# A scan layer with mixture-of-experts and flow attention: the first stage's order of work cut to single time steps

## The chip, the cores and the metric

The kernel runs on one core of one Trainium2 chip. The time is what the device needs for one execution, in microseconds (us). The kernel before takes 5714.69 us (median of 3 runs, 5713.19 to 5721.97). One further execution was recorded by the profiler; it took 5735.0 us, of which 5733.2 us lie between its first and its last instruction (the span). All rows quoted are from that execution.

The engines are named as the profile names them: PE is TensorE (PEld its weight loads), DVE VectorE, ACT ScalarE, POOL GpSimd, SP the engine whose queue issues the DMAs. [...]

## The reference

For x of 8 x 1024 x 256 in float32, four layers follow, each added to its input: a Mamba block, experts, a flow attention, and the same experts again. The first stage of the kernel computes the first two.

```python
xn = layernorm(x);  x_in, z = split(xn @ in_proj_w.T + in_proj_b)
x_conv = silu(causal_conv4(x_in))                  # 512 channels
Bm, Cm = split(x_conv @ x_proj_w.T + x_proj_b)     # 16 states each
delta  = clip(softplus(x_conv @ dt_proj_w.T + dt_proj_b), 1e-4, 10)
# for each time step t:
h = exp(clip(delta * A, -10, 0)) * h + delta * Bm * x_conv
# after every 16th step: h scaled down where its norm over the states is over 10
y = sum_n(Cm * h) + D_param * x_conv
out = layernorm(x + (y * silu(z)) @ out_proj_w.T + out_proj_b)
# experts: 16 of 256 x 256, the router's best 6 weighted, all 16 computed
out = sum_e(gate[:, e] * (tokens @ expert_w[e]))
```

## The kernel before

Stage one runs over 1024 time steps with all 8 batches at once. A partition holds one pair of batch and state (8 x 16 = 128), the free axis the 512 channels, so h is one tile of 128 x 512. The scan cannot be spread over time: each step (`step`, L545) is two instructions on DVE, `tmp = max(E, exp(-10)) * h` (L550) and `h = tmp + px` (L552). Everything else prepares or uses what the scan needs, and is woven between the steps:

- E = exp(delta * A). The deltas of 16 steps go to DRAM (L452, 256 KB) and come back spread over the states (`load_E`, 1 MB for a group of 4 steps, 3 buffers). POOL multiplies by A one step at a time (`mul_E`, L501) and ACT takes the exponential of four steps at once (`exp_E`, L505).
- px = B*u, one product per step with 32 rows (`inputs`, L537). The four steps of a group use four row groups of the array and four PSUM banks; a bank comes free when the step that reads it is done.
- py = C*h, four products per group in four column groups of the array, one bank (`outputs`, L581). `take_y` copies the bank out after 16 steps.
- after every 16th step the norm: ACT squares h, PE sums over the states, ACT takes logarithm and exponential, DVE scales h (`norm_a`, `norm_b`, `clip`).
- `pre(sc)` makes the inputs of the scan for a chunk of 32 steps (256 rows of tokens): normalisation, input projection, convolution, and the projections to B, C and delta; `gates(sc)` makes the gate z and both SiLUs, for which ACT loads another table. `weights(j)` builds the operands of B and C.
- `post(sc)` takes a finished chunk through the output projection, two normalisations and the router. `experts1(sc)` runs the 16 experts over both halves of the 256 tokens: two experts per PSUM bank (128 x 512, L707), read out by DVE (L727) for six of eight pairs and by ACT (L733) for two.

PSUM has 8 banks: four for px, one for py, and three that all other products share in turn (`psum()`, pool `ps_g`).

The order is written out by hand (`manual_schedule`). The main loop goes over groups of 4 steps; `PLAN` says after which step of which group of a chunk one part of the generators `ahead` (pre, letter a), `mid` (post, m) or `behind` (experts, b) is issued, and g calls `gates`. A generator's part ends at its `yield`. What a part issues goes to the end of each engine's queue, so a waiting instruction holds up all that its engine was given later. In the window from 200 to 3900 us 936 steps are recorded, 3.953 us a step or 126.5 us a chunk. Stage two (attention and the second experts) begins at about 4165 us and is not touched.

Of the kernel before, what the change touches and what calls it, by code (L numbers as in the profile page):

```python
# [17 lines left out]
P = 128  # L18
# [14 lines left out]
def tile_mamba_moe_flowattn_moe(ctx: ExitStack, tc: tile.TileContext, a: dict, out: bass.AP):  # L33
# [174 lines left out]
    with ExitStack() as ph:  # L208
# [8 lines left out]
        ps_g = ph.enter_context(tc.tile_pool(name="ps_g", bufs=3, space=PSUM))  # L217
# [115 lines left out]
        def pre(sc):  # L333
# [28 lines left out]
            for k in range(KD):  # L362
                for g in range(2):
                    nc.tensor.transpose(tp[:, k * 256 + g * P:k * 256 + (g + 1) * P],
                                        xn[:, g, k * P:(k + 1) * P], ident)
            xT = t["xT"] = io.tile([P, KD, HC + T * B], F32, tag="xT", name="xT")
# [12 lines left out]
            acc2 = t["acc"] = []  # L379
            prev = None  # L380
            for c in range(CB + 1):
                if c < CB:
                    ps = psum()
                    for k in range(KD):
                        nc.tensor.matmul(ps[:, 0:HC + T * B], inw[:, k, c * P:(c + 1) * P], xT[:, k, :],
                                         start=k == 0, stop=k == KD - 1)
                    if c % 2 == 0:
                        acc2.append(act.tile([P, 2, T * B], F32, tag="e", name="acc"))
                    acc = acc2[c // 2][:, c % 2, :]
                    nc.scalar.activation(acc, ps[:, 0:T * B], AF.Identity, bias=cbi[:, c:c + 1], scale=cw[:, c, 0:1])  # L390
                if prev is not None:
                    pps, pacc = prev
                    for k in range(1, 4):
                        nc.vector.scalar_tensor_tensor(pacc, pps[:, k * B:(k + T) * B], cw[:, c - 1, k:k + 1], pacc,  # L394
                                                       ALU.mult, ALU.add)
                    if sc == 0:
                        for i in range(3):
                            nc.vector.tensor_scalar(pacc[:, i * B:(i + 1) * B], pacc[:, i * B:(i + 1) * B],
                                                    cws[:, c - 1, 2 - i:3 - i], None, ALU.subtract)
                prev = (ps, acc)  # L400
                yield

            xc = t["xc"]
# [6 lines left out]
            dps = [psum(), None]  # L410
            for k in range(CB):
                nc.tensor.matmul(dps[0], tok(xc, k, 0), dtw[:, k, :], start=k == 0, stop=k == CB - 1)  # L412
            yield
            nc.vector.tensor_tensor(bc, bps[:, 0:4 * NS].rearrange("p (g n) -> p g n", g=2),
                                    xpb.unsqueeze(1).to_broadcast([P, 2, 2 * NS]), ALU.add)
            vs, es, ws = [], [], []
            for g in range(2):
                v = act.tile([P, DI], F32, tag="v", name="v")
                nc.vector.tensor_tensor(v, dps[g], dtb, ALU.add)
                e = act.tile([P, DI], F32, tag="e", name="e")  # L420
                nc.scalar.activation(e, v, AF.Abs)
                nc.scalar.activation(e, e, AF.Exp, scale=-1.0)
                w = act.tile([P, DI], F32, tag="w", name="w")
                nc.scalar.activation(w, e, AF.Identity, bias=1.0)
                vs.append(v), es.append(e), ws.append(w)
                if g == 0:
                    dps[1] = psum()
                    for k in range(CB):
                        nc.tensor.matmul(dps[1], tok(xc, k, 1), dtw[:, k, :], start=k == 0, stop=k == CB - 1)  # L429
                yield  # L430


            xcts = []
            for g in range(2):
                v, e, w = vs[g], es[g], ws[g]
# [3 lines left out]
                nc.vector.scalar_tensor_tensor(w, w, -1.0, e, ALU.add, ALU.subtract)  # L439
                nc.scalar.activation(e, e, AF.Ln, bias=1.0)  # L440
                nc.vector.scalar_tensor_tensor(v, v, 0.0, w, ALU.max, ALU.subtract)
                xct = act.tile([P, DI], F32, tag="xct", name="xct")
                nc.scalar.copy(xct, tp)
                xcts.append(xct)
                yield
            for g in range(2):
                v, e = vs[g], es[g]
                nc.gpsimd.tensor_tensor(v, v, e, ALU.add)
                nc.gpsimd.tensor_scalar(v, v, 10.0, 1e-4, ALU.min, ALU.max)
                c = ch_tiles[2 * sc + g] = {}  # L450
                c["dt"] = dbc.tile([4, B, QS, DI], F32, tag="dbc", name="dbc")
                nc.sync.dma_start(c["dt"].rearrange("q b tg d -> tg (q b) d"), v)  # L452
                yield
                u = c["u"] = act.tile([P, DI], F32, tag="u", name="u", bufs=3)
                nc.gpsimd.tensor_tensor(u, v, xcts[g], ALU.mult)
                if g == 1:
                    yield
# [5 lines left out]
        def gates(sc):  # L463

            t = sc_tiles[sc]
            xc = t["xc"] = act.tile([P, CB, 2, 4, 4, B], F32, tag="xc", name="xc")
            zs = t["zs"] = act.tile([P, CB, 2, 4, 4, B], F32, tag="zs", name="zs")
            zps = []
            for j in range(2):
                ps = psum()  # L470
                for i in range(2):
                    m = CB + 2 * j + i
                    for k in range(KD):
                        nc.tensor.matmul(ps[:, i * 256:(i + 1) * 256], inw[:, k, m * P:(m + 1) * P],
                                         t["xT"][:, k, HC:], start=k == 0, stop=k == KD - 1)
                zps.append(ps)
            acc = t.pop("acc")
            for dst, of, src in ((xc, lambda c: acc[c // 2][:, c % 2, :], "acc"),
                                 (zs, lambda c: zps[c // 2][:, c % 2 * 256:(c % 2 + 1) * 256], "z")):
                for c in range(CB):  # L480
                    for g in range(2):
                        nc.scalar.activation(
                            dst[:, c, g], of(c)[:, g * P:(g + 1) * P].rearrange("p (t4 tg b) -> p tg t4 b", t4=4, tg=4),
                            AF.Silu, bias=inb[:, CB + c:CB + c + 1] if src == "z" else 0.0)
            nc.scalar.preload_act_table_set("natural_log_exp_and_others")

# [4 lines left out]
        def load_E(G):  # L491
            if G < NQ:
                E_of[G] = scn.tile([P, QS, DI], F32, tag="E", name="E", bufs=3)
                j, q = divmod(G, 4)
                src = ch_tiles[j]["dt"][q].rearrange("b tg d -> b (tg d)")
                nc.sync.dma_start(E_of[G].rearrange("p tg d -> p (tg d)"),
                                  src.unsqueeze(1).to_broadcast([B, NS, QS * DI]))

        def mul_E(G, i):
            if G < NQ:  # L500
                nc.gpsimd.tensor_tensor(E_of[G][:, i, :], E_of[G][:, i, :], A_bn, ALU.mult)  # L501

        def exp_E(G):
            if G < NQ:
                nc.scalar.activation(E_of[G], E_of[G], AF.Exp)  # L505

        def weights(j):

            if j >= NQ // 4:
# [9 lines left out]
                                    bc[:, g, NS:].unsqueeze(1).to_broadcast([P, B, NS]), ALU.mult)  # L519
            ps = psum()  # L520
            nc.tensor.matmul(ps, cm.rearrange("p b n -> p (b n)"), sel.rearrange("p s t q b -> p (s t q b)"),
                             start=True, stop=True)
            lC = c["lC"] = scn.tile([P, 4, 4, 32], F32, tag="lC", name="lC")
            nc.scalar.copy(lC.rearrange("p q t m -> p (q t m)"), ps)

        def inputs(G):
# [6 lines left out]
            x_of[G] = []  # L533
            for tg in range(4):
# [3 lines left out]
                x_of[G].append(ps)  # L538
# [6 lines left out]
        def step(G, tg):  # L545
            if tg == 0:
                h_of[G] = []
            tmp = scn.tile([P, DI], F32, tag="tmp", name="tmp")

            nc.vector.scalar_tensor_tensor(tmp, E_of[G][:, tg, :], math.exp(-10.0), last[0], ALU.max, ALU.mult)  # L550
            h = scn.tile([P, DI], F32, tag="h", name="h", bufs=6)
            nc.vector.tensor_tensor(h, tmp, x_of[G][tg], ALU.add)  # L552
            h_of[G].append(h)
            last[0] = h
            if tg == 3:
                E_of.pop(G), x_of.pop(G)

        def norm_a(G):
            sq = scn.tile([P, DI], F32, tag="tmp", name="sq")
            nc.scalar.activation(sq, last[0], AF.Square)  # L560
            clips[G] = sq

        def norm_b(G):
# [3 lines left out]
            nc.tensor.matmul(ps, blk, sq, start=True, stop=True)  # L567
            nc.scalar.activation(sq, ps, AF.Ln, bias=tiny)
            nc.scalar.activation(sq, sq, AF.Exp, scale=-0.5, bias=ln10)

        def clip(G):
            nc.vector.scalar_tensor_tensor(last[0], clips.pop(G), 1.0, last[0], ALU.min, ALU.mult)  # L572
# [20 lines left out]
        def post(sc):  # L593
# [6 lines left out]
            tps = []  # L600
            for j in range(2):
                tp = psum()
                for i in range(2):
                    for g in range(2):
                        c = 2 * j + i
                        nc.tensor.transpose(tp[:, i * 256 + g * P:i * 256 + (g + 1) * P],
# [427 lines left out]
```

## Time and profile before

| | |
|---|---|
| median of 3 runs | 5714.69 us |
| profiled execution, its span | 5735.0 us, 5733.2 us |
| stage one, to the last store of `x2` | about 4165 us |
| PE, DVE, ACT, POOL busy over the span | 85%, 65%, 32%, 47% |
| granted TensorE clock over the span | 0.849 |

The page gives busy times per engine, the span in slices, the queues, the chain of work that ended last, and the groups of instructions. Busy time of PE is stretched where the granted clock is low: a matmul at half clock counts twice. The answers about waits name the waiting instruction, the one that released it, the sum, the number of times and the longest.

### The profile page before, as it was taken

Reading aid. Unit: us, or ns where it says so; the run is one execution under the profiler, and the core shown is the slowest. Engines: PE = TensorE matmul, PEld = TensorE weight load, DVE = VectorE, ACT = ScalarE, POOL = GpSimd, SP = SyncE. Lnnn points to the kernel's source line nnn. Section 1 sums busy time; section 2 is a strip of 40 time slices with the busy share of each in tenths; the row PEclk is TensorE's granted clock in tenths of the full one; section 3 lists DMA queues with packets and bytes.
Section 4 is the critical chain, followed back from the end, with each engine's and each line's share of the span. In section 5 each row is a group of like instructions: output and inputs, shape, how many; then the busy total and the mean of one; then the engine's idle time right before and its main releaser. Section 6 shows DMA issues by size and latency. Waiting matters only on the chain.

```text
span 5733.2 us, 47074 instructions
## 1 busy us (share of the span) xinstructions
PE 4864.5 (85%) x14024; PEld 2136.7 (37%) x14024; DVE 3731.1 (65%) x7655; ACT 1858.5 (32%) x3234; POOL 2684.9 (47%) x2431
## 2 busy tenths in 40 slices
PE   4788888888888888888888888888968889888999
PEld 2233333333333333333333333333334444444444
DVE  3677766666777676667776776676656665656563
ACT  3333333333333333333333333333222223222322
POOL 3555554555555555555555555555423333333333
PEclk7678788878887878878878887787989999999999
DMA  3333332333333333333333333333100000000000
GB/s 104 89 78 78 77 78 71 78 78 79 76 79 76 75 75 78 79 76 76 78 77 74 76 78 77 76 77 79 48 23 6 13 13 13 6 13 13 6 6 10
DMA packets 100926, 339.13 MB, mean 59 GB/s; under 512 B 11584, under 2 KB 58816, under 8 KB 67904
## 3 DMA queue, kind: packets, MB, share of 16 engines
q1 hardware_dynamic: 100672, 336.12, 23.9%
q8 instruction: 113, 1.85, 0.1%
q14 instruction: 141, 1.16, 0.1%
HBM read 302.54 MB, written 33.55 MB: 59 GB/s over the span
## 4 chain that ended last, share of the span: by engine, by line
PE 52%; DVE 30%; ACT 6%; issue 4%; POOL 4%; DMA 2%; SPq 1%; DVEq 0%; ACTq 0%; POOLq 0%
PE po L170 14%; PE pg L707 10%; DVE tmp L550 9%; DVE h L552 6%; PE px L537 6%; PE pg L412 3%; DVE o L727 2%; PE py L581 2%; ACT E L505 2%; PE mm L886 2%; PE pg L429 2%; PE mm L859 2%; DVE rc L913 2%; PE pg L625 1%; DVE acc L394 1%
## 5 line engine op out<-in xcount | busy, mean ns | idle before, releaser
L501 POOL TENSOR_TENSOR E<-E,A_bn 128x512 f32<-128x512 f32 x1024 | 1401.2, 1388 | 1001.9 <-DMA E<-dbc 870.9
L537 PE MATMUL px<-u,lB 32*128 32x512 f32 x2048 | 935.3, 785 | 423.6 <-DVE h L552 419.9
L707 PE MATMUL pg<-ew,xmT 128*128 128x512 f32 x2048 | 1154.9, 701 | 0.6 <-DVE o L727 0.6
L550 DVE SCALAR_TENSOR_TENSOR tmp<-E,h 128x512 f32<-128x512 f32 x1024 | 959.3, 937 | 27.5 <-ACT E L505 2.6
L170 PE MATMUL po<-ew,xmT 128*128 128x512 f32 x2048 | 914.9, 595 | 7.4 <-ACT sc__23342 L180 0.6
L552 DVE TENSOR_TENSOR h<-tmp,px 128x512 f32<-128x512 f32 x1024 | 703.8, 687 | 84.7 <-PE py L581 2.1
L707 PEld LDWEIGHTS pg<-ew,xmT 128*128 128x128 f32 x2048 | 441.7, 226 | 610.2 <-issue 597.8
L727 DVE SCALAR_TENSOR_TENSOR o<-pg,gt,o 128x256 f32<-128x256 f32 x768 | 369.5, 481 | 407.1 <-PE pg L707 393.2
L537 PEld LDWEIGHTS px<-u,lB 32*128 32x128 f32 x2048 | 247.6, 217 | 928.1 <-DVE h L552 803.0
L505 ACT ACTIVATE E<-E 128x2048 f32<-128x2048 f32 x256 | 486.9, 1902 | 294.6 <-POOL E L501 294.6
L170 PEld LDWEIGHTS po<-ew,xmT 128*128 128x128 f32 x2048 | 384.1, 191 | 459.1 <-issue 421.2
L174 DVE SCALAR_TENSOR_TENSOR x2t<-po,gt,x2t 128x256 f32<-128x256 f32 x512 | 244.3, 477 | 380.6 <-PE po L170 372.5
L581 PE MATMUL py<-h,lC 128*32 128x512 f32 x2048 | 377.0, 705 | 33.7 <-DVE h L572 33.7
L913 DVE RECIPROCAL rc<-mm 128x512 f32<-128x512 f32 x64 | 212.6, 3341 | 22.3 <-PE mm L859 22.3
L633 POOL TENSOR_TENSOR s<-s,phalf 128x2 f32<-128x2 f32 x32 | 34.2, 1070 | 375.1 <-DVE s L632 375.0
L394 DVE SCALAR_TENSOR_TENSOR acc<-pg,cw,acc 128x256 f32<-128x256 f32 x384 | 184.9, 482 | 21.8 <-ACT acc L390 12.7
L321 ACT ACTIVATE x<-xr,nb,r 128x256 f32<-128x256 f32 x64 | 35.0, 593 | 468.7 <-DVE nb L316 468.7
L581 PEld LDWEIGHTS py<-h,lC 128*32 128x32 f32 x2048 | 52.0, 118 | 341.6 <-issue 260.0
L620 POOL TENSOR_TENSOR x<-x,out_proj_b_r 128x512 f32<-128x512 f32 x32 | 40.9, 1278 | 292.5 <-ACT x L321 292.5
L859 PE MATMUL mm<-ke,wt 128*128 128x512 f32 x128 | 82.4, 781 | 108.3 <-DVE wt L856 101.6
L657 PE MATMUL pg<-rw,xmT 128*128 128x16 f32 x256 | 57.9, 366 | 131.5 <-ACT xmT L653 131.5
L79 DVE BATCH_NORM_STATS2 st<-o 128x6 f32<-128x256 f32 x128 | 52.6, 411 | 169.6 <-POOL o L639 168.5
(1066 smaller groups left out, 6465.8 us busy)
## 6 DMA issues: line engine op xcount, KB each, us to landing
E<-dbc SPq DMA_DIRECT2D x256, 1024.0 KB
dbc<-v SPq DMA_DIRECT2D x64, 256.0 KB
xt<-in_x_dram SPq DMA_DIRECT2D x256, 32.0 KB
xr<-in_x_dram SPq DMA_DIRECT2D x256, 32.0 KB
x<-o SPq DMA_DIRECT2D x256, 32.0 KB
x2t<-x SPq DMA_DIRECT2D x8, 1024.0 KB
out_dram<-x2t SPq DMA_DIRECT2D x32, 256.0 KB
ew<-in_expert_w_dram SPq DMA_DIRECT2D x2, 2048.0 KB
```

The costliest lines, as they stand in the source:

```text
L170: nc.tensor.matmul(po, xmT[:, k, g * P:(g + 1) * P], ew[:, k, 2 * j:2 * j + 2, :], start=k == 0, stop=k == KD - 1)
L174: nc.vector.scalar_tensor_tensor(xr[:, g, :], po[:, i, :], gt[:, g, 2 * j + i:2 * j + i + 1], xr[:, g, :], ALU.mult, ALU.add)
L394: nc.vector.scalar_tensor_tensor(pacc, pps[:, k * B:(k + T) * B], cw[:, c - 1, k:k + 1], pacc, ALU.mult, ALU.add)
L501: nc.gpsimd.tensor_tensor(E_of[G][:, i, :], E_of[G][:, i, :], A_bn, ALU.mult)
L505: nc.scalar.activation(E_of[G], E_of[G], AF.Exp)
L537: nc.tensor.matmul(ps, lB[r, q * P:(q + 1) * P], c["u"][r, :], start=True, stop=True)
L550: nc.vector.scalar_tensor_tensor(tmp, E_of[G][:, tg, :], math.exp(-10.0), last[0], ALU.max, ALU.mult)
L552: nc.vector.tensor_tensor(h, tmp, x_of[G][tg], ALU.add)
L581: nc.tensor.matmul(c["ps"][tg * 32:(tg + 1) * 32, :], c["lC"][:, q, tg, :], h_of[G][tg], start=q == 0, stop=q == 3)
L707: nc.tensor.matmul(po, xmT[:, k, g * P:(g + 1) * P], ew[:, k, 2 * j:2 * j + 2, :], start=k == 0, stop=k == KD - 1)
L727: nc.vector.scalar_tensor_tensor(o[:, g, :], po[:, i * D:(i + 1) * D], gt[:, g, 2 * j + i:2 * j + i + 1], o[:, g, :], ALU.mult, ALU.add)
L913: nc.vector.reciprocal(rc, ps)
```

## The change

The loop goes over time steps instead of groups of four. After each step one expert's product (128 x 256, two matmuls) and at most one short group of other products are issued, as a `PLAN` with one entry per step of a chunk says (a: pre of the next chunk, p: pre of the one after, m: post, w and W: weights, c: take_y, e: an expert, after every step).

- Experts: one per step, in turn in the two halves of a PSUM tile of its own, `pe` (one bank). The product of expert n is issued, then the read-out of expert n-1. The shared banks go from three to two. ACT reads out experts 4, 5, 10 and 11 of each half. The router's part moves from `experts1` into `post`.
- `inputs`: px of the last step of the next group is issued first. The pool hands out its four banks in the same turn as before, so this px takes the bank that the step just issued is still to read, and the other three wait behind it on PE.
- E in tiles of 2 steps (512 KB, 6 buffers): a load every second step, the multiplication 7 steps ahead (before: 6), the exponential of 2 steps, 4 steps ahead (before: 2).
- `gates` becomes part of `pre`; `pre`, `post` and `weights` get more and shorter parts. In `pre` the third and fourth input products are issued behind the convolution that frees their bank.
- The norm and the clip work in two halves of 256 columns.

```diff
+        ps_e = ph.enter_context(tc.tile_pool(name="ps_e", bufs=1, space=PSUM))
+        ps_g = ph.enter_context(tc.tile_pool(name="ps_g", bufs=2, space=PSUM))
+        pe = ps_e.tile([P, 2, D], F32, name="pe")
...
             for c in range(CB + 1):
+                if c > 0:
...
+                    nc.scalar.activation(acc, ps[:, 0:T * B], AF.Identity, bias=cbi[:, c - 1:c],
+                                         scale=cw[:, c - 1, 0:1])
+                    if prev is not None:
+                        conv(sc, c - 2, *prev)
+                    prev = (ps, acc)
                 if c < CB:
                     ps = psum()
...
+            for c in range(CB):
+                silu(xc, acc2[c // 2][:, c % 2, :], c, 0.0)
+            for c in range(CB):
+                silu(zs, zp[c // 2][:, c % 2 * 256:(c % 2 + 1) * 256], c, inb[:, CB + c:CB + c + 1])
+            nc.scalar.preload_act_table_set("natural_log_exp_and_others")
+            yield
...
-            for tg in range(4):
+            x_of[G] = {}
+            for tg in (3, 2, 1, 0):
                 ps = ps_x.tile([P, DI], F32, tag="x", name="px")
...
+            for n in range(2 * NE + 1):
+                g, e = divmod(n, NE)
+                if n < 2 * NE:
+                    po = pe[:, n % 2, :]
+                    for k in range(KD):
+                        nc.tensor.matmul(po, xmT[:, k, g * P:(g + 1) * P], ew[:, k, e, :],
+                                         start=k == 0, stop=k == KD - 1)
+                if before is not None:
+                    side = evict(o, gt, sm, side if e != 1 else None, *before)
...
+                before = (g, e, po)
+                yield
...
+        PLAN = ("cm", "m", "", "ma",
+                "a", "aa", "aW", "m",
+                "ma", "ma", "ma", "mw",
+                "mwa", "am", "a", "amp",
+                "ca", "am", "ap", "ap",
+                "a", "a", "p", "am",
+                "apW", "mw", "wm", "mp",
+                "mp", "mp", "mpp", "mp")
...
+            if t < L:
+                step(G, tg)
+            mul_E(t + 7)
+            if tg % 2 == 0:
+                exp_E(t // 2 + 2)
+            else:
+                load_E(t // 2 + 6)
+            if tg == 3:
+                if clipped:
+                    norm_a(G)
+                inputs(G + 1)
+                if clipped:
+                    norm_b(G)
+            for who in PLAN[n] + ("ee" if n == 31 else "e"):
...
+            if clipped:
+                clip(G)
+            if tg == 3 and G < NQ:
                 outputs(G)
```

## The prediction

> **What bounds the kernel now.** First the busy times by stretch, to see whether an engine is full. Columns: busy us of PE, PEld, DVE, ACT, POOL with counts, granted clock, DMA share, GB/s.
>
> ```profile
> 1000.00:2000.00 1000.00, 848.96 (x2460) 352.92 (x2460) 695.25 (x1295) 357.21 (x576) 543.69 (x432) 0.81 0.32 78
> 4600.00:5733.00 1133.00, 1033.75 (x2939) 513.62 (x2937) 622.18 (x1708) 293.13 (x660) 386.16 (x512) 0.96 0.03 10
> ```
>
> In stage one DVE is busy for 0.695 of the time: of the 126.5 us of a chunk 87.9 are work and 38.6 idle. PE looks fuller but runs at a mean clock of 0.81. So no engine is full; queues wait for each other. Next, what DVE waits for (window 200 to 3900, 29.25 chunks; us in total, times, longest):
>
> ```profile
> DVE o L727 <- PE pg L707: 347.2, 97, 6.7
> DVE st L79 <- POOL o L639: 157.4, 29, 6.7
> DVE bc L414 <- PE pg L408: 156.2, 29, 6.5
> DVE v L419 <- PE pg L412: 134.5, 29, 5.5
> DVE lg L660 <- PE pg L657: 115.0, 29, 4.0
> DVE h L572 <- ACT sq L569: 53.4, 30, 4.2
> ```
>
> Per chunk: 11.9 us for experts' products, 19.3 for the next four together, 1.8 for the clip, some 5.6 in gaps. The scan itself (L550, L552) waits for E or px hardly at all. Third, the clock, in windows of 3.41 us:
>
> ```profile
> 2010.02:2013.44 3.42, 1.89 (x10) 0.80 (x8) 3.30 (x7) 0.90 (x2) 0.00 (x0) 1.00 0.18 57
> 2013.44:2016.85 3.41, 3.41 (x10) 0.95 (x12) 3.31 (x5) 1.94 (x4) 2.94 (x3) 0.53 0.52 111
> 2091.94:2095.36 3.42, 1.60 (x7) 0.34 (x5) 3.22 (x3) 0.93 (x3) 2.71 (x2) 1.00 0.49 108
> 2095.36:2098.77 3.41, 3.41 (x11) 2.06 (x11) 3.17 (x6) 1.69 (x1) 0.00 (x0) 0.53 0.40 99
> 2218.24:2221.65 3.41, 2.15 (x10) 0.40 (x9) 2.68 (x2) 1.07 (x3) 3.38 (x3) 1.00 0.48 113
> 2221.65:2225.06 3.41, 2.70 (x11) 1.35 (x12) 3.10 (x6) 2.38 (x2) 0.29 (x1) 1.00 0.37 102
> ```
>
> After a window with 1.60 or 1.89 us of PE work the clock halves for the next one; after 2.15 it stays. In the chain of waits:
>
> ```profile
> 2023.60 1.81 PE px L537 x2
> 2043.67 3.73 PE pg L707 x4
> 2063.58 3.41 PE pg L707 x4
> 2143.09 3.01 PE pg L707 x4
> ```
>
> Four matmuls of L707 take about 1.75 us at full clock and a px 1.12. Adding up what such pieces lose in the chunk from 2023.6 to 2150.5 gives 13.8 us. At full clock the chunk would need about 113.
>
> **Edits with one answer.** E moves the same bytes. ACT does 512 exponentials of 1024 columns for 256 of 2048: rows of 0.63 us (512 columns) and 1.90 (2048) leave a fixed 0.20, so 256 x 0.20 = 51 us on ACT, which is idle 65%; without that cover 51 us. SP issues 256 more loads of 0.61 us, 156 us on a queue that stood 2224 us waiting for a scan step to free an E buffer. The queue also carries the moved loads of x (8 behind step 15, 8 behind step 0), the stores of x2 (behind 16 and 31, waiting for POOL) and the deltas (behind 18 and 24). 8 loads have taken 15 us behind an E load; such a hold delays E. Behind it stand POOL's multiplications, but loads now lead them by 4 steps (before 3) and the scan by 11, and 512 KB take half of today's 8.5 us. I take nothing; uncovered it is one late load a chunk, some 5 us. The clip in halves costs DVE the same (0.96 us against two of 0.48).
>
> An expert takes 4 matmuls of 256 columns. Stage two has that shape: 37.8 us for 160 of L900, 0.236 each, 0.945 an expert, against 4 x 0.446 / 2 = 0.89 by L170 (704.6 for 1579). 1024 experts x 0.05 = 56 us on PE, behind DVE's work; uncovered 56. PE's work at full clock is some 80 us a chunk.
>
> **What it removes.** The four DVE waits of 19.3 us a chunk: each reader now comes in a later step than its product. About 2 may stay: -17.3. **px:** four together have taken 1.14 us (like a pair), apart 3.65 a group on average (935.3 / 256). That is PE time, which bounds nothing by itself; but all four now start only after the group's last h.
>
> **What it adds: the coupling of PE and DVE.** An eviction today reads one of three rotating banks; no row shows DVE reading a bank that PE has next to write. The nearest row is L552 on its own four banks, with 0.08 us of idle a step. The Trainium skill (*PSUM — Partial Sum Buffer*, "PSUM bank collisions raise a hardware error") says that two engines must be kept apart by bank and quadrant, not by address. `pe` is one bank. So I take it that the program makes read-out n-1 wait for product n, issued just ahead of it, and product n+1 for that read-out. Each wait is zero or the excess of PE's path over DVE's own work; scan step 1.65 us (0.94 + 0.69), eviction 0.5, expert to readable result 1.09 (0.945 + 0.15 tail), semaphore 0.05.
>
> - A fourth step, behind 19: h at 1.65, px holds PE to 2.66, the delta product 0.88, expert 1.09, 0.05: 4.68. DVE has 1.65 + 1.4. Wait 1.6. Likewise behind 3, 15, 23 and 31 (with their norms and products): 1.05, 0.7, 2.5, 0.3. Sum 6.2.
> - The step after, behind 8: PE is free 0.25 late (py 0.95), then L625 0.94, L408 1.0, expert 1.09, 0.05 = 3.33 against 1.65: 1.7. Behind 0, 4, 9, 13, 16, 20: 1.1, 0.7, 0.7, 1.75, 0.45, 0.65. Sum 7.05.
> - Two shared banks: the third input product waits for the convolution of the same step (DVE 1.65 + 1.6 + 1.45 = 4.7), then 0.94 + 1.09 + 0.05 = 6.8: wait 2.1 behind 29, 1.15 behind 30.
> - Behind 6, ACT gets 16 SiLUs and two table loads, 6.4 us in the row of before, ahead of the read-out of expert 5. Product 7 waits for that read-out, every DVE read-out behind it: 6.3 us. The same rows already held up L408 today.
>
> Sum 22.9 in place of 11.9. The chunk at full clock is 87.9 + 22.9 + 2 + 1.8 + about 3.6 of gaps = 118. If the halves were independent, the first three would shrink to about 3 and the SiLUs' to 6: 104. I take the whole wait, by the rule, with 104 as the other end.
>
> **The clock after.** PE's work is spread more evenly, but five stretches of a chunk stay thin: behind steps 1 to 2 (2.5 us of work in 8), 6 to 7, 17 to 18, 29 to 30 and 31. What follows runs at half clock: px, a product and an expert lose about 1.0 + 0.9 + 1.0, some on cover; I take 2.2 each, 11 us. The skill (*TensorE: Matmul & The Clock Gate*, Part 1) has the clock halved after an idle window of about 3.4 us. The window fits, but the rows above halve after 1.60 and 1.89 us of work. By the page only a pause as long as a window costs, almost nothing here: 118 a chunk. By the rows 118 + 11 = 129, which I take.
>
> **Sum.** 129 - 126.5 = +2.5 us over 30 chunks with experts: +75. After the scan 64 steps remain with experts alone. They took about 95 us (4064 to 4159). Now product and read-out alternate, at best 1.09 + 0.05 + 0.5 = 1.65, at half clock up to 2.7; at 1.95 it is 125: +30. 5735 + 105 = 5840 for the profiled execution. The median lies 0.35% below it: **5820 us**, 1.8% slower. 0.2% is about what a measurement of this kernel can tell from no change.
>
> **Rivals.**
> 1. Slower, as above: chance 0.56. Its own range is 5730 to 6010: 6010 if every thin stretch halves the clock on the path (some 134 a chunk: +225, and +50 at the end).
> 2. The clock holds, as the page has it, and the removed waits win: 118 + 3 = 121 a chunk, -5.5 x 30 + 30 = -135: 5580. For it: an expert behind every step leaves no long pause. Against it: the threshold near 2 us of 3.41 in the rows. It decides once the half-clock loss falls below 7 us a chunk. Chance 0.28.
> 3. No wait by bank: 104 + 6 = 110, -16.5 x 30 = -495: 5220. For it: nothing in the profile is against it. Against it: the rule. Chance 0.12.
> 4. The gains and the new waits cancel within 0.2%: 5703 to 5726, 126.5 less 1 a chunk for the longer end. Chance 0.04.
>
> So faster 0.40, same 0.04, slower 0.56. Cases of both signs hold most of the chance, so the range reaches into rival 2 and to the edge of 3: 5380 to 6000, leaving about 0.11 below and 0.08 above.
>
> **What the changed profile would show.** Right: DVE's waits for bc, v, lg and st near zero; evictions waiting for the experts' product about 23 us a chunk or more, largest behind every fourth step and around the SiLUs; px in fours of 1.14 or 2.08 us behind h; a clock of about 0.85 in stage one; POOL seldom waiting for E. Wrong: evictions that hardly wait (rival 3), or a clock above 0.95 (rival 2). E arriving late, or DVE's own rows lengthening, would break the sum elsewhere.

## The result and the profile after

The changed kernel takes **5934.34 us** (median, 5926.35 to 5940.5), the kernel before 5716.88 us beside it: a ratio of 1.038 (95% interval 1.0361 to 1.0397), so 3.8% slower. The forecast was 5820 us, 1.8% slower: the right side, about half the size. The profiled execution took 5940.5 us (span 5938.8), 205.5 us more than before's 5735.0.

Where they lie: the last clip of the scan ends at 4245.0 us (before 4090.6), and stage two's first work on DVE starts at 4375.6 (before 4170.3). So the scan takes 154.4 us longer and the tail of experts behind it 50.9 us (130.6 for 79.7). Together they are the whole difference. From first to last h the scan takes 129.3 us for 32 steps, before 124.5.

What DVE waits for, in the same window as before (200 to 3900 us; us in total, times, longest):

```profile
DVE o L759 <- PE pe L743: 975.4, 376, 8.0
DVE top L711 <- ACT lg L703: 49.8, 27, 3.4
DVE s L357 <- POOL s L355: 30.6, 28, 1.1
DVE h L575 <- PE px L559: 18.1, 36, 1.3
DVE st L79 <- POOL o L674: 10.0, 23, 0.4
```

The four waits that the change was to remove (bc, v, lg, st: 563 us together) are gone but for some 16 us, most of it at st; new ones, for the exponential of the router's logits (top) and for POOL (s), are 80. The wait for experts' products rose from 347 to 975 us. In this window 897 steps are recorded, 132.0 us a chunk, of which these waits are 34.8.

The clock, in windows of 3.41 us. Columns: busy us of PE, PEld, DVE, ACT, POOL with counts, granted clock, DMA share, GB/s.

```profile
2016.85:2020.26 3.41, 1.72 (x8) 1.05 (x6) 3.38 (x5) 1.06 (x1) 3.41 (x4) 1.00 0.15 45
2020.26:2023.67 3.41, 3.41 (x8) 1.29 (x8) 3.34 (x7) 0.00 (x0) 1.43 (x1) 0.61 0.21 65
2023.67:2027.09 3.42, 3.42 (x7) 1.68 (x6) 0.81 (x2) 0.00 (x0) 0.00 (x0) 0.50 0.52 128
2027.09:2030.50 3.41, 3.41 (x18) 1.95 (x17) 2.02 (x3) 0.00 (x0) 2.11 (x2) 0.89 0.53 131
```

One thin window (1.72 us of PE work) is followed by some 7 us at half clock. Six stretches at half clock, of 3.4 to 10.2 us, lie between 2013 and 2144 us; stage one's mean clock is 0.83 (before 0.81). The work alone does not decide it: here is a fuller window, mostly px with its 32 rows, and the one behind it.

```profile
2065.39:2068.80 3.41, 2.82 (x10) 0.91 (x9) 3.08 (x5) 0.23 (x1) 3.33 (x3) 1.00 0.01 2
2068.80:2072.21 3.41, 3.41 (x6) 1.63 (x6) 3.10 (x8) 0.49 (x2) 3.29 (x4) 0.50 0.47 126
```

The timeline around the longest wait of that chunk, behind step 6 (start, duration, engine, line; in brackets the idle time ahead and who ended it):

```profile
2039.55 1.13 PE L658 MATMUL pg<-outw,yT 128*128 128x256 f32 x4 [1.54 <-ACT zs L406]
2042.37 2.07 PE L743 MATMUL pe<-ew,xmT 128*128 128x256 f32 x4 [1.69 <-ACT side L764]
...
2041.84 0.47 ACT L764 ACTIVATE side<-pe,gt 128x256 f32<-128x256 f32 x1
...
2044.48 0.48 DVE L759 SCALAR_TENSOR_TENSOR o<-pe,gt,o 128x256 f32<-128x256 f32 x1 [7.57 <-PE pe L743]
```

ACT's read-out stands behind the SiLUs, product 7 behind it, and DVE behind the product for 7.57 us. But PE itself stood at the product for only 1.69 us: until shortly before, it had waited for the SiLUs in another place (L658, for the bank of z).

### The profile page after: what moved, and what is told of

Read it like the earlier page. It is cut to its first block, busy times and chain, and to the rows that moved or that the text cites. A ratio compares the mean times of both kernels' runs of the same rounds, so it can differ in the third digit from the quotient of the medians.

```text
span 5938.8 us, 52317 instructions
## 1 busy us (share of the span) xinstructions
PE 4924.3 (83%) x16200; PEld 2544.5 (43%) x16200; DVE 3790.6 (64%) x7719; ACT 1918.4 (32%) x3682; POOL 2758.0 (46%) x2431
## 5 line engine op out<-in xcount | busy, mean ns | idle before, releaser
L743 PE MATMUL pe<-ew,xmT 128*128 128x256 f32 x4096 | 1280.9, 442 | 292.5 <-DVE o L759 166.1
L743 PEld LDWEIGHTS pe<-ew,xmT 128*128 128x128 f32 x4096 | 859.6, 222 | 718.1 <-DVE o L759 302.0
L759 DVE SCALAR_TENSOR_TENSOR o<-pe,gt,o 128x256 f32<-128x256 f32 x768 | 369.4, 481 | 1156.1 <-PE pe L743 1154.9
L559 PE MATMUL px<-u,lB 32*128 32x512 f32 x2048 | 817.1, 801 | 122.1 <-DVE h L575 119.4
L523 ACT ACTIVATE E<-E 128x1024 f32<-128x1024 f32 x512 | 537.6, 1051 | 201.8 <-POOL E L519 201.8
L750 POOL TENSOR_TENSOR o<-o,side 128x256 f32<-128x256 f32 x128 | 122.3, 956 | 538.3 <-DVE o L759 531.9
L448 PE MATMUL pg<-dtw,xc 128*128 128x512 f32 x512 | 328.3, 732 | 2.6 <-DVE v L457 2.3
L764 ACT ACTIVATE side<-pe,gt 128x256 f32<-128x256 f32 x192 | 90.9, 473 | 736.2 <-PE pe L743 735.8
L399 PE MATMUL pg<-xT,inw 128*128 128x280 f32 x512 | 190.6, 506 | 162.4 <-DVE acc L477 156.8
L399 PEld LDWEIGHTS pg<-xT,inw 128*128 128x128 f32 x512 | 106.2, 229 | 239.8 <-issue 135.3
L658 PE MATMUL pg<-outw,yT 128*128 128x256 f32 x512 | 165.4, 453 | 45.8 <-ACT zs L406 45.8
L477 DVE SCALAR_TENSOR_TENSOR acc<-pg,cw,acc 128x256 f32<-128x256 f32 x384 | 182.5, 482 | 22.3 <-ACT acc L391 13.2
```

Of the source, the lines that this page charges most:

```text
L448: nc.tensor.matmul(ps, tok(xc, k, g), dtw[:, k, :], start=k == 0, stop=k == CB - 1)
L523: nc.scalar.activation(E_of[H], E_of[H], AF.Exp)
L559: nc.tensor.matmul(ps, lB[r, q * P:(q + 1) * P], c["u"][r, :], start=True, stop=True)
L743: nc.tensor.matmul(po, xmT[:, k, g * P:(g + 1) * P], ew[:, k, e, :], start=k == 0, stop=k == KD - 1)
L759: nc.vector.scalar_tensor_tensor(o[:, g, :], po, gt[:, g, e:e + 1], o[:, g, :], ALU.mult, ALU.add)
```

## The experiments

Times are medians; ratios are to the kernel before on the same chip.

### The order of read-out and product

```diff
+                if before is not None:
+                    side = evict(o, gt, sm, side if e != 1 else None, *before)
...
                 if n < 2 * NE:
                     po = pe[:, n % 2, :]
                     for k in range(KD):
                         nc.tensor.matmul(po, xmT[:, k, g * P:(g + 1) * P], ew[:, k, e, :],
                                          start=k == 0, stop=k == KD - 1)
-                if before is not None:
-                    side = evict(o, gt, sm, side if e != 1 else None, *before)
```

> The kernel after with one edit: in each experts' step the read-out of expert n-1 is issued ahead of the product of expert n. PE's order and DVE's order among their own instructions stay as they are. Theory A (the two halves of the one bank share one order of accesses, so read-out n-1 waits for product n): the wait of the read-outs falls from 36 us a chunk to about 7 (the one behind the SiLU block stays, since product 6 then waits for ACT's read-out of expert 5), 29 us x 30 chunks = 870: about 5065 us, 5000 to 5250. The last 64 steps, which alternate in either order, stay at about 131 us. Theory B (the halves are independent and PE is simply late by its own queue, half clock above all): read-out n-1 waited for product n-1, which stands where it stood; 5900 to 5960.

Measured: **5342.84 us**, ratio 0.9349 (0.9328 to 0.9371). Two statements exchanged are worth 592 us, and the kernel is now faster than before. From first to last h it takes 110.6 us a chunk for 129.3. The wait (200 to 3600 us, 972 steps, so 13.2 us a chunk):

```profile
DVE o L759 <- PE pe L751: 400.2, 198, 8.2
```

Theory A holds and B falls: PE's order against its other work is the same, only the product that a read-out waits for is one step older. The gain is smaller than forecast: 13.2 us of waits a chunk are left and not 7, and DVE's own work rose from 90.1 to 93.2 us a chunk. Half of the waits left is the hold behind the SiLUs, now in full:

```profile
2013.57 2.07 PE L751 MATMUL pe<-ew,xmT 128*128 128x256 f32 x4 [5.87 <-ACT side L764]
2015.76 0.48 DVE L759 SCALAR_TENSOR_TENSOR o<-pe,gt,o 128x256 f32<-128x256 f32 x1 [6.42 <-PE pe L751]
```

The profiled execution of this kernel took 5386.6 us and the others 5341 to 5347: its tail behind the scan took 173 us, from 3679 us on at a granted clock of 0.50. More on that below.

### Which experts ACT reads out

```diff
-            if e not in (4, 5, 10, 11):
+            if e not in (1, 2, 9, 10):
...
```

> The kernel after with one edit: ACT reads out experts 1, 2, 9 and 10 of each half in place of 4, 5, 10 and 11, so that none of its read-outs stands behind the 16 SiLUs and two table loads. Theory A: the hold behind the SiLUs (7.6 us in the chunk looked at, 6.3 in the forecast) goes from each of 30 chunks: 190 to 220 us, so 5715 to 5745. Rival: PE is held behind the SiLUs anyway, because the products of B, C and delta need xc, so the wait only moves: 5890 to 5940.

Measured: 5915.89 us, ratio 1.0366 (1.0332 to 1.0400), which can't be told from after. The rival holds: no read-out stands behind the SiLUs now, and DVE waits as long in other places (992.8 us in 876 steps from 300 to 3900 us, where after has 975.4 in 864). With the read-out first and the tail mended it is different (below): there the same edit is worth 122 us.

### The tail in four banks

```diff
-                    po = pe[:, n % 2, :]
+                    po = ps_x.tile([P, DI], F32, tag="x", name="px")[:, 0:D] if now[0] >= L else pe[:, n % 2, :]
...
```

> The kernel after with one edit: the experts of the 64 steps behind the scan (t from 1024 on) write in turn to the four px banks, which are free by then, in place of the two halves of pe. Theory A: product and read-out no longer alternate; the tail goes from about 131 us to the 80 us of the kernel before, or somewhat more: 5880 to 5895 us. Rival: the tail is bound by PE at half clock whatever the bank: 5925 to 5945.

Measured: 5888.88 us, ratio 1.0298 (1.0274 to 1.0323): 45 us less, and the tail takes 80.1 us (before 79.7). The alternation of product and read-out in `pe` is the whole of what the tail lost. The px tiles differ from the halves of `pe` in two ways, as banks and as tiles; which of the two makes the program tie product and read-out together, no run tells apart.

### px in its old order, in both kernels

```diff
-            for tg in (3, 2, 1, 0):
+            for tg in (0, 1, 2, 3):
```

> The kernel after with one edit: px of the next group is issued in the order 0, 1, 2, 3 again, as before. Since the pool hands out the bank that came free first, the first three px of either order take banks that are already read, and the last waits for the group's last h in both: my reading of the trace is no change by more than 0.3% (5915 to 5955). Rival (the reversed order is what makes PE run the four side by side): px come apart again, 2.5 us of PE for each of 8 groups in a chunk, a third to all of it on the path of the fourth steps: 6130 to 6500.

Measured: 5954.91 us, ratio 1.0424 (1.0399 to 1.0449): 21 us more than after, so the reversed order helps a little or nothing (the intervals just part). The reverse edit in the kernel before:

> The kernel before with one edit: px of a group issued in the order 3, 2, 1, 0. The pool hands out the bank that came free first, so three px can start at once and the last, which is the one that the next step needs first, waits for the group's last h. In the kernel before the first px is issued behind that h too, but needs only the first bank. Expected: PE runs the four more closely (less than the 3.65 us a group of before), the step behind a group gets its px up to 1 us later, hidden or not: 5690 to 5800, most likely within 0.5% of before.

Measured: 5724.6 us, ratio 1.0008 (0.9993 to 1.0023): nothing.

### E by pairs of steps

The loads, the multiplication and the exponential as before, the rest as after:

```diff
...
-            mul_E(t + 7)
-            if tg % 2 == 0:
-                exp_E(t // 2 + 2)
-            else:
-                load_E(t // 2 + 6)
+            mul_E(t + 6)
+            if tg == 2:
+                exp_E(G + 1)
+            elif tg == 3:
+                load_E(G + 3)
```

> The kernel after with one part undone: E again in tiles of four steps (1 MB loads, 3 buffers, multiplication 6 steps ahead, exponential of four steps at once, issued behind the third step of a group). Everything else as after. The forecast took E by pairs at nothing, so 5920 to 5950. Rival 1 (256 more exponentials and loads cost their 51 us on the path): 5880 to 5900. Rival 2 (the longer lead of E by pairs is needed with one step at a time, or an exponential of 1.9 us holds up read-outs of ACT): 5960 to 6100.

Measured: **5846.71 us**, ratio 1.0202 (1.0182 to 1.0222). The part that the forecast took at nothing costs 88 us. None of the three expectations has this size. Which half of it? First the loads alone, two of 512 KB for each buffer of 1 MB, then the exponentials and the longer lead alone:

> As e7_E_fours (exponential of four steps at once, three buffers of 1 MB), but each buffer filled by two loads of 512 KB, so as many loads as in the kernel after. If the 88 us that E by pairs costs lie with ACT's 256 more exponentials or their places in its queue: as e7_E_fours, 5830 to 5870. If they lie with SP's 256 more loads or the smaller transfers: as after, 5915 to 5955.

Measured: 5926.56 us (ratio 1.0358, 1.0328 to 1.0388), 80 of the 88.

> As e7_E_fours in its loads (1 MB, three buffers), as the kernel after in its arithmetic (multiplication 7 steps ahead, exponential of two steps every second step). In e12_fours_two_loads the loads alone, halved, brought back 80 of the 88 us. If loads and exponentials add: as e7_E_fours plus some 8 us, 5840 to 5870. If the cost comes from E being ready early, whatever makes it so, this kernel has it too in part: 5880 to 5940.

Measured: 5891.1 us (ratio 1.0286, 1.0262 to 1.0310), 44 of the 88. The halves don't add up: either alone brings back half or more. So it is no price per load or exponential. The profiled executions (after 5940.5 us, fours 5876.2, two loads 5929.5, pairs of exponentials 5915.8) show where each loses, from 200 to 3900 us, in us a chunk:

| | chunk | DVE's own work | its waits for products | its wait for POOL at st | mean clock |
|---|---|---|---|---|---|
| after | 132.0 | 90.1 | 34.8 | 0.4 | 0.83 |
| E by fours | 129.8 | 89.9 | 32.9 | 0.4 | 0.83 |
| fours, two loads | 131.7 | 91.4 | 33.4 | 0.2 | 0.82 |
| fours, pairs of exponentials | 130.8 | 90.9 | 30.2 | 2.8 | 0.85 |

The lines of the products' waits with fours, and of the wait that only the last kernel has at this size:

```profile
DVE o L757 <- PE pe L741: 937.3, 375, 9.1
```

```profile
DVE st L79 <- POOL o L673: 80.2, 27, 4.4
```

Against E by fours, after loses 1.9 us a chunk in waits for products, the kernel with two loads mostly in longer instructions of DVE, the last one in waiting for POOL. With smaller loads POOL waits less for E (in after 268 us, with fours 541, before 769), so more of its instructions can stand beside others of DVE. One such place in after: POOL multiplies without a pause, from 2013.70 on five steps in a row, beside the 1.37 us in which DVE gates y at step 1. With E by fours POOL waits there for its load, and the same instruction takes 0.69:

```profile
2013.70 8.00 POOL L519 TENSOR_TENSOR E<-E,A_bn 128x512 f32<-128x512 f32 x5
...
2017.51 1.37 DVE L636 TENSOR_TENSOR yT<-yT,zs 128x512 f32<-128x512 f32 x1
...
2019.33 1.13 PE L743 MATMUL pe<-ew,xmT 128*128 128x256 f32 x4 [1.69 <-DVE o L759]
```

PE then idles 1.69 us for the read-out (1.00 with fours). But over the whole window this instruction takes 1.02 us on average in after and 1.05 with fours, where the other of the two in a chunk is the long one, and half clock follows behind this place in both. So the place is an example and not the account of the 88 us.

### More work for PE

The result of a product is written a second time in the thin stretches, behind the read-out of the expert before:

```diff
+                if n in (1, 2, 6, 14, 17, 21, 29, 30) and now[0] < L:
+                    for k in range(KD):
+                        nc.tensor.matmul(po, xmT[:, k, g * P:(g + 1) * P], ew[:, k, e, :],
+                                         start=k == 0, stop=k == KD - 1)
...
```

> The kernel after, with the product of experts 1, 2, 6, 14, 17, 21, 29 and 30 of every chunk issued once more behind the read-out of the expert before (the same result again): 8 x 0.945 = 7.6 us more of PE work a chunk in the thin stretches that I find in the trace of after. In the chunk from 2013 to 2144 us six stretches of 6.8 to 10.2 us run at half clock. By the forecast's reading of the rows (a window with less than about 2 us of PE work in 3.41 halves the clock; worth 11 us a chunk) the granted clock rises from 0.83 to 0.9 or more and the time falls by up to 8 us a chunk: 5700 to 5900. If the halving costs little on the path, or isn't avoided: 5930 to 6170.

Measured: 5895.65 us, ratio 1.0304 (1.0262 to 1.0346). The clock of stage one rose from 0.83 to 0.90, and a kernel that does 7.6 us more of PE work a chunk became 39 us faster, 1.3 us a chunk. Both kernels from 200 to 3900 us, first after, then this one:

```profile
200.00:3900.00 3700.00, 3041.58 (x10526) 1593.41 (x10524) 2525.17 (x4627) 1316.62 (x2426) 1959.89 (x1506) 0.83 0.27 74
```

```profile
200.00:3900.00 3700.00, 2852.38 (x11536) 1639.85 (x11534) 2597.38 (x4676) 1332.47 (x2456) 1983.52 (x1518) 0.90 0.27 75
```

PE ran 10% more matmuls in 6% less busy time. And E by fours with the same added work:

> As e11_after_more_work (eight products of a chunk issued once more, granted clock 0.90), with E in tiles of four steps as in e7_E_fours. If E by pairs costs its 88 us by way of the clock (PE thinner ahead of the fourth steps, then px and product at half clock), little of it is left once the clock is held: 5870 to 5910, as e11_after_more_work. If it costs them in another way: 5795 to 5825.

Measured: 5877.25 us, ratio 1.0276 (1.0246 to 1.0307), 18 us under the run above, with intervals that overlap. With the added work E by pairs costs 18 us or nothing in place of 88. That does not show that half clock is the way by which it costs them: the mean clock is the same 0.83 in after and with E by fours, and the kernel with fours and pairs of exponentials has the higher clock, 0.85, and is 44 us slower than with fours alone. The added work made the kernel with fours 31 us slower and after 39 us faster; why, no run here shows.

### Towards a faster kernel

The read-out first and the tail in four banks:

> Two edits on the kernel after: the read-out of expert n-1 ahead of the product of expert n (as in e1_readout_first) and the last 64 steps through the four px banks (as in e3_tail_banks). In e1_readout_first the scan's part is 110.6 us a chunk, but the tail takes 173 us, all of it at a granted clock of 0.50: each read-out and product alternate there with a period of 2.65 us. With the banks in turn the tail should fall to the 80 us of e3_tail_banks: 93 us less, 5240 to 5265 us. Rival (the half clock, once begun, stays whatever the banks): 5300 to 5345.

Measured: 5297.48 us, ratio 0.9247 (0.9229 to 0.9265). The expectation of 5240 to 5265 was made from the execution with the slow tail; against the median it is 45 us less, as in after.

And ACT on experts 1, 2, 9 and 10:

> As e5_first_tail, and ACT reads out experts 1, 2, 9 and 10 in place of 4, 5, 10 and 11. In the kernel after, that edit alone gave 18 us, since PE reached the held product only 1.7 us before ACT's read-out; with the read-out first PE stands 5.9 us there. So here the hold should go: 5.9 us a chunk x 30 = 180 us less than e5_first_tail, about 5070. Rival: the wait moves to other read-outs as it did in e2_act_experts: within 40 us of e5_first_tail.

Measured: **5175.35 us**, ratio 0.9038 (0.9023 to 0.9053), the fastest kernel of this study. The hold is worth 122 us here, against 18 in after; 274.7 us of waits for experts are left from 300 to 3500 us. Two further edits on it:

> As e6_first_tail_act, and the products of experts 1, 2, 16, 17, 19, 28 and 29 of every chunk are issued twice (the second writes the same result again): 7 x 0.945 = 6.6 us more of PE work a chunk, placed where the granted clock of e6_first_tail_act falls to half for 7 to 10 us at a time. If work holds the clock up: a mean granted clock in stage one above 0.96 (0.925 without), and what half clock costs on the path, at most e6's 9.2 us of waits a chunk, comes back in part: 5000 to 5150 us. If the halving doesn't depend on the work of the window before: clock as without, and up to 6.6 us a chunk more: 5180 to 5380 us.

Measured: 5225.78 us, ratio 0.9135 (0.9105 to 0.9166). The clock rose from 0.92 to 0.95, and the time with it: with most waits gone, the added work costs more than the higher clock gives.

> As e6_first_tail_act, with E in tiles of four steps again, as in e7_E_fours. If the 88 us that this gave there are ACT's 51 us of fixed cost and what hangs on it, they come off here too in part: 5080 to 5130 us. If they were tied to the waits of read-outs for products, which are mostly gone here: 5160 to 5200. If the shorter lead now starves the faster scan of E: 5200 to 5350.

Measured: 5413.05 us, ratio 0.9464 (0.9438 to 0.9489). In the faster scan E by pairs, 88 us too dear in after, is worth 238. ACT waits 492 us for POOL's multiplications there, and scan steps for ACT and px 163 us (from 300 to 3500 us; 5.9 us a chunk, 1.4 without the edit). DVE's own work is 3.7 us a chunk longer too (96.4 for 92.7).

## Why the prediction was right in its direction and half the size

**The coupling by the bank** was the main step, and the order of the two statements shows it. The prediction took the whole wait, by the rule that two engines are kept apart by bank; rival 3 (independent halves) is out. In the window of the forecast the experts' waits are 34.8 us a chunk, forecast 22.9 + 11 = 33.9 (the terms listed add up to 22.8). So close an agreement is in part luck: its clock part was not found at that size, and its SiLU part is no term that can be added (both below).

**The chunk** was forecast at 129 us and took 132.0 in the same window. By terms: DVE's own work is 90.1 us a chunk, not 87.9 (+2.2); the waits for products are 0.9 longer; what is left of the removed waits, with the new ones for top and s, is about 3 us, not 2; and the wait at the clip, which the sum kept at 1.8 us, is gone. The forecast's own working (129 less 126.5, 30 chunks) gave +75; the scan lost 154.4.

**The step that failed** is that the sum put two costs of the scan at nothing: E by pairs ("I take nothing") and any lengthening of DVE's own work. E by pairs, undone, is 88 us; in the profiled executions it is 2.2 us a chunk, 1.9 of them in waits for products. DVE's work is 2.2 us a chunk above the sum's value (1.9 above the kernel before in the same window, 88.2), an estimated 66 us over 30 chunks: small instructions of two columns, of which some took 0.15 to 0.16 us before and now stand beside POOL's. This is a term of its own, since with E by fours they are as long. Against both stands the clip's wait; the scan was under-forecast by 79 us. For E by pairs the cover that the prediction named (ACT idle, SP idle, a longer lead) was there, and POOL did wait less. The uncovered price that it gave (51 us on ACT, or one late load) describes another mechanism. How E by pairs costs its 88 us stays open: the three kernels that have a part of it lose in three different places, and the mean clock does not tell them apart.

**The tail** was to go from 95 to 125 us. It went from 79.7 to 130.6: 95 was read from the wrong end of the scan (4064 us; the last clip ends at 4090.6), and the growth was 21 us more than forecast.

**The SiLU term** of 6.3 us was no term of a sum. The wait is there (7.57 us in the chunk shown), but PE came to the product only 1.69 us before ACT freed it, and taking the hold away gave 18 us, which can't be told from nothing. Only with the larger wait removed did it count. The same holds for the list of waits at single steps: they are of the right sum, but not added independently.

**The clock term** of 11 us a chunk is shown in its direction (more work, higher clock), not in its size. Filling the thin stretches gives 1.3 us a chunk net of the work added. The threshold near 2 us of work was read from three windows and does not hold over all of them. Counted in step with the clock's records from 200 to 3900 us: under 1.6 us of PE work, every window at full clock was followed by half clock (55 before, 100 after); of those with 2.2 to 2.9 us, 48 of 69 before and 70 of 241 after, most of them filled with px; from 3.0 us on, 2 of 440 and none of 264. Half clock ended only behind windows with more than 3.0 us. These counts are not the rule that rival 2 took from the page, a whole idle window, and rival 2 (the clock holds) is out with 0.83.

**px** was described wrongly, in the account of the change ("the other three wait behind it") and in "all four now start only after the group's last h". The weight loads below fit a pool that hands out the bank that came free first: two px can start at once, one waits for the step before the last, and only px of step 0, issued last, waits for the last h (two loads belong to one px):

```profile
2020.39 0.30 PEld L559 LDWEIGHTS px<-u,lB 32*128 32x128 f32 x4 [0.33 <-issue]
2021.34 0.50 PEld L559 LDWEIGHTS px<-u,lB 32*128 32x128 f32 x2 [0.65 <-DVE h L575]
2023.05 0.49 PEld L559 LDWEIGHTS px<-u,lB 32*128 32x128 f32 x2 [1.21 <-DVE h L575]
```

The path of the fourth step, which the sum used, ends the same: the last px behind h. The order is worth 21 us in after and nothing in the kernel before.

## What to carry to other kernels

Where two engines alternate on one PSUM bank, it is the order of issue, not the number of halves, that makes a double buffer: read out the old result before the next product is issued. Waits that lie one behind the other on coupled queues don't add up, and an edit's worth depends on what else stands beside it: taking the SiLU hold away gave 122 us or nothing that could be measured, and undoing E by pairs gave 88 us or cost 238. So the parts of a change are best measured on the version in which the largest wait is already gone. A part that only brings data earlier is not free: ask beside what the earlier engine will then run.

## What the hardware showed

**One loop, two speeds.** In the tail a product and its read-out alternate. In after each round takes 1.71 us at full clock; in the profiled execution of the kernel with the read-out first, 2.65 us at half clock, for over 100 us. First a stretch of after, then of the other:

```profile
4296.00:4358.00 62.00, 41.24 (x153) 25.67 (x152) 16.08 (x47) 4.96 (x11) 5.43 (x6) 1.00 0.02 4
```

```profile
3690.24:3741.43 51.19, 41.58 (x90) 25.44 (x88) 9.40 (x33) 3.84 (x8) 2.71 (x3) 0.50 0.01 3
```

PE is busy for 2.27 us of 3.41 in the first and 2.77 in the second, but the second's work is worth half at full clock, 1.39 us. Either speed lasted through its stretch. It fits the counts above: in stage one half clock ended only behind windows with more than 3.0 us of PE work, and the slow loop has 2.77. PE pauses for at most 1.1 us in either stretch. The tails of that kernel's faster executions are not recorded.

**Small DVE instructions beside POOL.** The shift for a normalisation, two columns, before and after:

```profile
L316 DVE SCALAR_TENSOR_TENSOR nb<-mv,rm 128x2 f32<-128x2 f32 x29 | 4.4, 153 | 0.0
```

```profile
L319 DVE SCALAR_TENSOR_TENSOR nb<-mv,rm 128x2 f32<-128x2 f32 x28 | 32.9, 1175 | 0.0
```

From 153 to 1175 ns. In eight chunks in the middle of the scan it begins in after 0.51 us into a multiplication of POOL and ends 0.02 us behind it, 1.21 us later; in before nothing of POOL runs beside it. The Trainium skill (*SBUF — State Buffer*, "SBUF: two separate sides") has DVE, with two inputs from SBUF, and POOL share a pair of ports, which the one that starts first holds for its whole instruction; these rows agree.
